# Two layers of graph attention with norms: bank copies, norms and statistics in another order in the first steps and in the tail

## The chip, the cores and the metric

The kernel runs on one core of a Trainium2 chip. The metric is the device time in microseconds (us) of that core, as a median of several runs. TensorE (PE in the profile) multiplies matrices, VectorE (DVE), ScalarE (ACT) and GpSimd (POOL) compute elementwise, and SyncE (SP) issues nearly all transfers (DMAs) between SBUF and DRAM. PE writes its products to banks of a memory called PSUM; the other engines read them from there.

## The reference

The input x has 128 batch elements of 128 rows and 512 columns, in fp32. Cut to what matters, with adj used as both weights of layer 0:

```python
A = einsum('od,bdn->bon', adj, x); C = A + b
x = layernorm(x + max(relu(A[:, :, None, :] + (C - A)[:, :, :, None]), axis=-1))
q, k, v = split_heads(x @ w_qkv)            # 8 heads of 64
attn = softmax(where(adj == 0, -inf, q @ k.T / 8))
o = (attn @ v) @ w_proj + b_proj
ln = layernorm(o) * gamma + beta
out = layernorm(x + o + ln)
```

In layer 0, C - A is the bias alone, so the kernel needs only the row maximum of adj @ x, plus bias, with relu, added to x.

## The kernel before, in words

Two batch elements make a pair and a step; four make a group (G = 4, 32 groups of 512 rows). All arithmetic is in fp32. The three large products (q and k, v, the projection) are made by a scheme of seven block products in place of eight for a pair of 2 by 2 blocks. `Unit` (L153) holds one such product: `product(i)` issues the 8 matmul instructions in the profile of product i into one of four PSUM banks b1 to b4. Products 1, 6 and 7 accumulate in b1; `snap(k)` (L171) copies b1 to SBUF on ACT after each of them, and the next product into b1 waits for that copy. `result(half, col)` (L176) adds a snap and a bank on DVE: (0, 0) takes b2 and snap 1, (0, 1) b3 and snap 2, (1, 1) b3 and snap 3, (1, 0) b4 and snap 3. Product 5 opens b3 and product 3 adds to it, so product 3 waits until result (1, 1) has read b3, and the next unit's product 5 waits until result (0, 1) has read it.

Every instruction is issued in the order in which the code is written (`tc.keep_in_program_order`, L71): each engine has one queue in that order, and an instruction waits at its head until all that it needs is done. There is no scheduler; the order is written out by hand. The helpers `pe` (L73) and `tt` (L76) record all matmuls under L74 and all elementwise two-operand operations under L77.

Layer 0 for element f: `l0_mm` (adjacency matmul into a whole bank), `l0_max` (DVE maximum and r), `l0_add` (ACT), statistics, `l0_norm` (ACT). `bn` (L233) makes two DVE instructions per element, L235 and L236. `finish_stats` (L238) makes one DVE instruction (sh, L244) and three on POOL: variance plus epsilon (L246), a power of -0.5 which gives rs, and the product of sh and rs. `normalize` (L252) is one ACT instruction, L254, that needs both. `stats` (L603) does bn for each item and one finish for all. The normed x is transposed in 32 by 32 blocks on DVE (`l0_transpose`), written to DRAM and read back in another order (`l0_write`, `l0_read`: four SP transfers each; `xhop`, `x1T`), gets beta added on POOL (`l0_beta`) and is spilled to DRAM for the end.

Attention for element b: `scores` (PE), `softmax_max` (DVE), `softmax_exp` (ACT, one head at a time), `softmax_div` and `prob_transpose` (DVE, tiles s and pu), `prob_write` and `prob_read` (SP: one write to `hop`, four reads into pT), `attend` (PE, into banks po and pa), `attend_copy` (ACT, to oT).

The first steps, L612 to L697, are written out: the units qk(0, 0), called `before` from L656 on, and qk(0, 1), called `cur` from L659, with the layer 0 work of elements 4 to 9. The loop at L706 takes p from 0 to 60. Step p makes a unit `first` and a unit `second`, layer 0 for later pairs, attention for pair p, and the tail of earlier pairs; p = 0 has branches of its own, where `first` is the v unit of group 0.

After the loop (L860 on) the rest is written out, with L = 127 the last element. Its last lines, L934 to L1030, are the tail of the last elements. The tail for element t on the usual way: `tail_inner_one` (L580, ACT norm of o), `tail_residual_one` (L584, three POOL operations: times gamma, plus o, plus the spilled x), statistics of z, and `tail_outer_one` (L598, ACT norm and the store). `tail_fused` (L589) replaces inner norm and residual by three DVE instructions, L594, L595 and L77, of which the second needs rs. For L - 3 to L, o is left in PSUM by `last_project` (L499); o of the others lies in SBUF. Before, L - 3 to L take the fused way and L - 11 to L - 4 the usual one.

Of the kernel before, what the change touches and what calls it, by code (L numbers as in the profile page):

```python
# [16 lines left out]
def kernel(  # L17
# [35 lines left out]
    G = 4  # L53
    GT = G * P
    HT = GT // 2
    HE = D // 2
# [28 lines left out]
    def broadcast(queue, name, src):  # L85
        t = const.tile([P, D], F32, name=name)
        pin(queue.dma_start(out=t, in_=src.partition_broadcast(P)))
        return t
# [26 lines left out]
    def weight_sums(w, cols, width):  # L115
        t = w[:, :, :, ds(cols, width)]
        b11, b21, b22, b12 = (t[:, i] for i in range(4))
        tt(nc.gpsimd, t[:, 4], b12, b11, ALU.subtract)
        tt(nc.gpsimd, t[:, 6], b22, b12, ALU.subtract)
        tt(nc.gpsimd, t[:, 5], b22, t[:, 4], ALU.subtract)  # L120
        tt(nc.gpsimd, t[:, 3], b21, t[:, 5], ALU.subtract)
# [111 lines left out]
    def bn(src, mv, k):  # L233
        st = small.tile([P, 6], F32, tag="st", name=f"st_{k}_{mv.name}")
        pin(nc.vector.bn_stats(st, src))  # L235
        pin(nc.vector.bn_aggr(mv[:, k], st))  # L236
# [37 lines left out]
    def l0_norm(f):  # L274
        normalize(xs[f], xs[f], ("y", f))
# [133 lines left out]
    def softmax_div(b):  # L409
        rec = small.tile([P, H], F32, tag="rec", name=f"rec_{b}")  # L410
        pin(nc.vector.reciprocal(rec, psums.pop(b)))  # L411
        p = prob[b]
        tt(nc.vector, p, p, rec.unsqueeze(2).to_broadcast([P, H, P]), ALU.mult)
# [52 lines left out]
    def attend_copy(b):  # L466
        g, h, jj = place(b)
        if jj == 0:
            tag = "x" if (g, h) == (NG - 2, 0) else "oT"
            oT[g, h] = sb.tile([P, KC, HT], F32, tag=tag, name=f"oT_{g}_{h}", bufs=2)  # L470
        pin(nc.scalar.copy(oT[g, h][:, :, ts(jj, P)], pos.pop(b)))
# [45 lines left out]
    def o_of(b):  # L517
        g, h, jj = place(b)
        return os_[b] if b in os_ else os_[g, h][:, jj]
# [60 lines left out]
    def tail_inner_one(b):  # L580
        z_tile(b)
        normalize(zs[b], o_of(b), ("o", b))
# [20 lines left out]
    def stats(name, *items):  # L603

        mv = small.tile([P, NC, 2], F32, tag="mv", name=f"mv_{name}")
        for k, (kind, b) in enumerate(items):
            bn({"o": o_of, "z": zs.get, "y": xs.get}[kind](b), mv, k)
        finish_stats(mv, items)
        return mv
# [51 lines left out]
    weight_load(wp, w_proj, 0, HE, 0, HE)  # L661
    ga_bc = broadcast(nc.sync, "ga_bc", ln_gamma)
    bp_bc = broadcast(nc.sync, "bp_bc", b_proj)
    before.snap(3)
    before.result(1, 1)
    before.result(1, 0)
    stats("second", *(("y", f) for f in range(G, 2 * G)))
    weight_sums(wv, 0, HE)
    for f in range(G, G + 2):
        l0_norm(f)  # L670
    cur.product(2)
    cur.product(1)
    cur.snap(1)
    cur.result(0, 0)
    before.product(3)
    before.result(0, 1)
    for f in range(G + 2, 2 * G):
        l0_norm(f)
    cur.product(6)
    cur.snap(2)  # L680
    cur.product(5)
# [24 lines left out]
    for p in range(LAST + 1):  # L706
# [7 lines left out]
        keys = []  # L714
# [79 lines left out]
            l0_read(n)  # L794
        if p > 0:
            first.snap(3)
        softmax_div(b)
        prob_transpose(b)
        prob_write(b)
        prob_read(a)  # L800
        prob_read(b)
        first.result(1, 1)
        first.result(1, 0)
        if ph == 1 and tb is not None:
            one("z", zs, tb)
        if ph == 0 and ta is not None:
# [53 lines left out]
    L = B - 1  # L860
# [101 lines left out]
    o_u.result(0, 0)  # L962
    v_u.product(3)
    v_u.result(0, 1)
    for t in range(L - 11, L - 7):
        tail_residual_one(t)
    o_u.product(6)
    softmax_exp(L, range(4))
# [14 lines left out]
    tail_outer(B // 2 - 7)  # L983
    tail_store(B // 2 - 7)
    mv = small.tile([P, NC, 2], F32, tag="mv", name="mv_last_2")
    keys = [("z", L - 11), ("z", L - 10), ("o", L - 5), ("o", L - 4), ("o", L - 7), ("o", L - 6)]
    bn(zs[L - 11], mv, 0)
    bn(zs[L - 10], mv, 1)
    o_u.result(1, 1)
    o_u.result(1, 0)  # L990
    bn(o_of(L - 5), mv, 2)
    bn(o_of(L - 4), mv, 3)
    o_u.product(3)
    o_u.result(0, 1)
    last_project(L - 3, wlast, "b2")
    last_project(L - 2, wlast, "pss0")
    attend(L - 1)
    attend_copy(L - 1)
    attend(L, "pa")
    attend_copy(L)  # L1000
    last_project(L - 1, wlast, "pss1")
    last_project(L, wlast, "b1")
    bn(o_of(L - 7), mv, 4)
    bn(o_of(L - 6), mv, 5)
    finish_stats(mv, keys)
    for t in (L - 5, L - 4, L - 7, L - 6):
        tail_inner_one(t)
    for t in (L - 11, L - 10):
        tail_outer_one(t)
    tail_residual_one(L - 5)  # L1010
    mv = stats("last_3", ("o", L - 3), ("o", L - 2), ("z", L - 9), ("z", L - 8))
    tail_residual_one(L - 4)
    for t in (L - 9, L - 8):
        tail_outer_one(t)
    tail_fused(L - 3, mv[:, 0, 0:1])
    tail_fused(L - 2, mv[:, 1, 0:1])
    mv = stats("last_4", ("o", L - 1), ("z", L - 3), ("z", L - 2))
    tail_residual_one(L - 7)
    tail_fused(L - 1, mv[:, 0, 0:1])
    for t in (L - 3, L - 2):  # L1020
        tail_outer_one(t)
    mv = stats("last_5", ("o", L), ("z", L - 5), ("z", L - 4))
    tail_residual_one(L - 6)
    tail_fused(L, mv[:, 0, 0:1])
    for t in (L - 5, L - 4):
        tail_outer_one(t)
    stats("last_6", ("z", L - 1), ("z", L - 7))
    stats("last_7", ("z", L), ("z", L - 6))
    for t in (L - 1, L - 7, L, L - 6):
        tail_outer_one(t)  # L1030


# [39 lines left out]
```

## Time and profile before

| what | value |
|---|---|
| median of 3 runs | 1987.33 us (1987.06 to 1987.37) |
| profiled execution, its own time | 1988.53 us |
| span of that execution | 1986.7 us |
| PE busy | 1946.4 us (98%) |
| DVE busy | 1565.2 us (79%) |
| POOL busy | 1293.7 us (65%) |
| ACT busy | 1055.1 us (53%) |
| PE in the chain that ended last | 95% |

Times in the trace count from the start of the span. A timeline row gives start, length, engine, line, operation, output and inputs, count, and in brackets how long the engine was idle before it and which instruction released it. Rows of several instructions are merged, so a length can hold small gaps. `SPq` is SP's own queue: the length is that of issuing, not of the transfer. The span is a little shorter than the execution's own time, which also holds what lies around the span.

### The profile page before, as it was taken

What the parts mean: (1) busy time and instruction counts of PE and PEld (TensorE: products, weight loads), DVE (VectorE), ACT (ScalarE), POOL (GpSimd) and SP (SyncE); (2) the same over time, 40 slices, a digit from 0 to 9 for tenths busy, and PEclk for the clock granted to TensorE, in tenths of its full rate; (3) what the DMA queues carried; (4) which work ended last, traced back from release to release, by engine and by line L of the source; (5) the groups of instructions that cost most, each with busy time, mean ns of one, the idle gap of its engine ahead of it and who ended that gap; (6) DMA issues with size and microseconds to landing.
All of it is one profiled execution on the core that took longest, in us unless ns stands there. A gap on an engine that the chain in (4) does not pass through costs nothing.

```text
span 1986.7 us, 33036 instructions
## 1 busy us (share of the span) xinstructions
PE 1946.4 (98%) x11545; PEld 1644.8 (83%) x11545; DVE 1565.2 (79%) x2518; ACT 1055.1 (53%) x3066; POOL 1293.7 (65%) x808
## 2 busy tenths in 40 slices
PE   7999999999999999999999999999999999999994
PEld 5888888888888888888888888888888888888872
DVE  5668788788788788787787787787787787787685
ACT  3435546546556556555555555555455455455453
POOL 5246667677667677667676667676667676676646
PEclk8999999999999999999999999999999999999997
DMA  5665576675675675765766765765766766765553
GB/s 191 145 170 139 159 195 155 181 195 153 183 187 158 186 187 157 187 170 169 192 168 169 194 165 164 202 165 164 202 159 168 198 164 165 198 162 158 159 177 121
DMA packets 445655, 341.76 MB, mean 172 GB/s; under 512 B 276912, under 2 KB 378416, under 8 KB 445488
## 3 DMA queue, kind: packets, MB, share of 16 engines
q1 hardware_dynamic: 445056, 338.85, 64.1%
q8 instruction: 92, 1.51, 0.3%
q10 hardware_dynamic: 432, 0.79, 0.1%
q14 instruction: 75, 0.61, 0.1%
HBM read 172.82 MB, written 166.72 MB: 171 GB/s over the span
## 4 chain that ended last, share of the span: by engine, by line
PE 95%; DVE 2%; DMA 1%; POOL 1%; ACT 0%; issue 0%; SPq 0%; ACTq 0%; POOLq 0%; DVEq 0%
PE b_qk L74 39%; PE b_v L74 19%; PE b_o L74 19%; PE pss L74 6%; PE po L74 6%; PE pa L74 5%; PE pp L74 0%; POOL zl L77 0%; DMA x<-in_x_dram 0%; DMA wqk<-in_L_gnn_w_qkv_dram 0%; DVE s_x L77 0%; DMA hop<-pu 0%; DVE st_mv_last L235 0%; DVE z L77 0%; POOL rs_mv_last L77 0%
## 5 line engine op out<-in xcount | busy, mean ns | idle before, releaser
L74 PE MATMUL b_qk<-s_x,wqk 128*128 128x256 f32 x2048 | 476.3, 381 | 4.0 <-ACT u_qk L173 3.9
L74 PEld LDWEIGHTS b_qk<-s_x,wqk 128*128 128x128 f32 x2048 | 391.8, 191 | 58.1 <-POOL wv L77 4.3
L400 ACT ACTIVATE s<-s,nmax 128x128 f32<-128x128 f32 x1024 | 396.2, 391 | 6.7 <-DVE nmax L393 6.7
L74 PE MATMUL b_qk<-x1T,wqk 128*128 128x256 f32 x1536 | 360.7, 385 | 0.8 <-DVE x1T L299 0.8
L74 PEld LDWEIGHTS b_qk<-x1T,wqk 128*128 128x128 f32 x1536 | 288.7, 191 | 45.5 <-DVE x1T L299 1.2
L77 POOL TENSOR_TENSOR z<-z,ga_bc 128x1024 f32<-128x1024 f32 x58 | 164.6, 2838 | 168.4 <-ACT z L254 168.4
L246 POOL TENSOR_SCALAR rs_mv<-mv 128x6 f32<-128x6 f32 (+2 forms) x61 | 14.6, 240 | 380.2 <-DVE mv L236 380.2
L77 DVE TENSOR_TENSOR s<-s,rec 128x1024 f32<-128x1024 f32 x128 | 252.3, 1971 | 4.4
L173 ACT COPY u_qk<-b_qk 128x512 f32<-128x512 f32 x192 | 112.3, 585 | 248.2 <-PE b_qk L74 247.2
L74 PE MATMUL b_v<-wv,s_x 128*128 128x256 f32 x1024 | 237.2, 380 | 2.0 <-DVE v L179 2.0
L74 PE MATMUL b_o<-wp,s_o 128*128 128x256 f32 x992 | 230.2, 380 | 0.5 <-DVE v L179 0.5
L74 PEld LDWEIGHTS b_v<-wv,s_x 128*128 128x128 f32 x1024 | 194.8, 190 | 28.7 <-DVE v L179 2.4
L179 DVE TENSOR_TENSOR qk<-b_qk,u_qk 128x512 f32<-128x512 f32 x256 | 168.1, 675 | 62.2 <-PE b_qk L74 44.6
L381 DVE SCALAR_TENSOR_TENSOR s<-pss,mask 128x512 f32<-128x512 f32 x256 | 164.3, 684 | 59.5 <-PE pss L74 59.1
L74 PEld LDWEIGHTS b_o<-wp,s_o 128*128 128x128 f32 x992 | 188.5, 190 | 26.7 <-DVE v L179 0.9
L77 POOL TENSOR_TENSOR x<-x,be_bc 128x1024 f32<-128x1024 f32 x64 | 182.1, 2847 | 34.0 <-DVE rec L411 27.6
L400 ACT ACTIVATION_READ_ACCUMULATOR s<-s,nmax 128x1 f32 x1024 | 194.2, 190 | 0.0
L179 DVE TENSOR_TENSOR v<-b_v,u_v 128x512 f32<-128x512 f32 x128 | 87.0, 681 | 133.6 <-PE po L74 128.8
L173 ACT COPY u_o<-b_o 128x512 f32<-128x512 f32 x93 | 54.4, 585 | 247.3 <-PE b_o L74 247.3
L173 ACT COPY u_v<-b_v 128x512 f32<-128x512 f32 x96 | 56.2, 585 | 238.5 <-PE b_v L74 238.5
L74 PE MATMUL b_v<-wv,x1T 128*128 128x256 f32 x768 | 176.3, 379 | 0.0
L74 PEld LDWEIGHTS b_v<-wv,x1T 128*128 128x128 f32 x768 | 146.3, 190 | 31.9 <-issue 13.8
(107 smaller groups left out, 3395.5 us busy)
## 6 DMA issues: line engine op xcount, KB each, us to landing
hop<-pu SPq DMA_DIRECT2D x128, 512.0 KB, 3.5
pT<-hop SPq DMA_DIRECT2D x512, 128.0 KB, 3.7
spill<-x SPq DMA_DIRECT2D x64, 512.0 KB, 4.8
x<-in_x_dram SPq DMA_DIRECT2D x62, 512.0 KB, 4.4
xhop<-xt SPq DMA_DIRECT2D x248, 128.0 KB, 2.3
x1T<-xhop SPq DMA_DIRECT2D x248, 128.0 KB, 3.9
xr<-spill SPq DMA_DIRECT2D x59, 512.0 KB, 3.6
out_dram<-xr SPq DMA_DIRECT2D x58, 512.0 KB, 4.1
```

Of the source, the lines that this page charges most:

```text
L74: pin(nc.tensor.matmul(*args, **kwargs))
L77: pin(eng.tensor_tensor(dst, a, b, op))
L173: pin(nc.scalar.copy(t, self.banks[1]))
L179: nc.vector.tensor_tensor(self.out[half, col], self.banks[bank], self.snaps[k], ALU.add)
L246: pin(nc.gpsimd.tensor_scalar(rs[:, :n], mv[:, :n, 1], EPS, None, ALU.add))
L381: nc.vector.scalar_tensor_tensor(s[:, par], pss[b][par], SCALE, mask.unsqueeze(1).to_broadcast([P, NP, P]), ALU.mult, ALU.add,)
L400: nc.scalar.activation(prob[b][:, i], prob[b][:, i], AF.Exp, bias=nmax[b][:, i : i + 1], accum_out=psums[b][:, i : i + 1],)
```

## The change

In the first steps, the statistics of elements 4 to 7 and the sums of the v weights move ahead of the old unit's last copy and two results; the four norms of these elements, which stood two by two ahead of the copies `cur.snap(1)` and `cur.snap(2)`, now stand together between these copies. At p = 0, results (1, 1) and (1, 0) of the v unit move ahead of the softmax divisions, behind which they stood.

In the tail, elements L - 4 and L - 6 go from the usual way to the fused one, so that six elements take it in place of four. Residual L - 8 moves behind the first finish. The statistics are finished in seven portions of 4, 3, 3, 3, 4, 1 and 2 columns in place of six of 6, 4, 3, 3, 2 and 2. The inner norms of L - 5 and L - 7 and the outer ones of L - 11, L - 10 and L - 9 stand ahead of the attention copies of L - 1 and L on ACT; all of these stood behind the copies before. The order on PE is the same in both kernels; that on SP differs only in the order and tiles of the last stores.

```diff
--- before.py
+++ after.py
@@ -661,21 +661,19 @@
     weight_load(wp, w_proj, 0, HE, 0, HE)
     ga_bc = broadcast(nc.sync, "ga_bc", ln_gamma)
     bp_bc = broadcast(nc.sync, "bp_bc", b_proj)
+    stats("second", *(("y", f) for f in range(G, 2 * G)))
+    weight_sums(wv, 0, HE)
     before.snap(3)
     before.result(1, 1)
     before.result(1, 0)
-    stats("second", *(("y", f) for f in range(G, 2 * G)))
-    weight_sums(wv, 0, HE)
-    for f in range(G, G + 2):
-        l0_norm(f)
     cur.product(2)
     cur.product(1)
     cur.snap(1)
     cur.result(0, 0)
     before.product(3)
+    for f in range(G, 2 * G):
+        l0_norm(f)
     before.result(0, 1)
-    for f in range(G + 2, 2 * G):
-        l0_norm(f)
     cur.product(6)
     cur.snap(2)
     cur.product(5)
@@ -794,13 +792,17 @@
             l0_read(n)
         if p > 0:
             first.snap(3)
+        else:
+            first.result(1, 1)
+            first.result(1, 0)
         softmax_div(b)
         prob_transpose(b)
         prob_write(b)
         prob_read(a)
         prob_read(b)
-        first.result(1, 1)
-        first.result(1, 0)
+        if p > 0:
+            first.result(1, 1)
+            first.result(1, 0)
         if ph == 1 and tb is not None:
             one("z", zs, tb)
         if ph == 0 and ta is not None:
@@ -962,7 +964,7 @@
     o_u.result(0, 0)
     v_u.product(3)
     v_u.result(0, 1)
-    for t in range(L - 11, L - 7):
+    for t in range(L - 11, L - 8):
         tail_residual_one(t)
     o_u.product(6)
     softmax_exp(L, range(4))
@@ -983,50 +985,51 @@
     tail_outer(B // 2 - 7)
     tail_store(B // 2 - 7)
     mv = small.tile([P, NC, 2], F32, tag="mv", name="mv_last_2")
-    keys = [("z", L - 11), ("z", L - 10), ("o", L - 5), ("o", L - 4), ("o", L - 7), ("o", L - 6)]
+    keys = [("z", L - 11), ("z", L - 10), ("o", L - 5), ("o", L - 4)]
     bn(zs[L - 11], mv, 0)
     bn(zs[L - 10], mv, 1)
     o_u.result(1, 1)
     o_u.result(1, 0)
     bn(o_of(L - 5), mv, 2)
     bn(o_of(L - 4), mv, 3)
+    finish_stats(mv, keys)
+    tail_inner_one(L - 5)
+    for t in (L - 11, L - 10):
+        tail_outer_one(t)
+    tail_residual_one(L - 8)
     o_u.product(3)
     o_u.result(0, 1)
     last_project(L - 3, wlast, "b2")
     last_project(L - 2, wlast, "pss0")
     attend(L - 1)
+    attend(L, "pa")
+    mv2 = stats("last_3", ("o", L - 7), ("o", L - 6), ("z", L - 9))
+    tail_inner_one(L - 7)
+    tail_outer_one(L - 9)
+    tail_residual_one(L - 5)
+    tail_fused(L - 4, mv[:, 3, 0:1])
     attend_copy(L - 1)
-    attend(L, "pa")
     attend_copy(L)
     last_project(L - 1, wlast, "pss1")
     last_project(L, wlast, "b1")
-    bn(o_of(L - 7), mv, 4)
-    bn(o_of(L - 6), mv, 5)
-    finish_stats(mv, keys)
-    for t in (L - 5, L - 4, L - 7, L - 6):
-        tail_inner_one(t)
-    for t in (L - 11, L - 10):
+    mv = stats("last_4", ("o", L - 3), ("z", L - 8), ("z", L - 4))
+    tail_residual_one(L - 7)
+    for t in (L - 8, L - 4):
         tail_outer_one(t)
-    tail_residual_one(L - 5)
-    mv = stats("last_3", ("o", L - 3), ("o", L - 2), ("z", L - 9), ("z", L - 8))
-    tail_residual_one(L - 4)
-    for t in (L - 9, L - 8):
+    tail_fused(L - 6, mv2[:, 1, 0:1])
+    mv2 = stats("last_5", ("o", L - 2), ("z", L - 6), ("z", L - 5))
+    tail_fused(L - 3, mv[:, 0, 0:1])
+    for t in (L - 6, L - 5):
         tail_outer_one(t)
-    tail_fused(L - 3, mv[:, 0, 0:1])
-    tail_fused(L - 2, mv[:, 1, 0:1])
-    mv = stats("last_4", ("o", L - 1), ("z", L - 3), ("z", L - 2))
-    tail_residual_one(L - 7)
+    tail_fused(L - 2, mv2[:, 0, 0:1])
+    mv = stats("last_6", ("o", L - 1), ("z", L - 3), ("z", L - 2), ("z", L - 7))
+    for t in (L - 3, L - 2, L - 7):
+        tail_outer_one(t)
+    mv2 = stats("last_7", ("o", L))
     tail_fused(L - 1, mv[:, 0, 0:1])
-    for t in (L - 3, L - 2):
-        tail_outer_one(t)
-    mv = stats("last_5", ("o", L), ("z", L - 5), ("z", L - 4))
-    tail_residual_one(L - 6)
-    tail_fused(L, mv[:, 0, 0:1])
-    for t in (L - 5, L - 4):
-        tail_outer_one(t)
-    stats("last_6", ("z", L - 1), ("z", L - 7))
-    stats("last_7", ("z", L), ("z", L - 6))
-    for t in (L - 1, L - 7, L, L - 6):
+    tail_fused(L, mv2[:, 0, 0:1])
+    stats("last_8", ("z", L - 1), ("z", L))
+    for t in (L - 1, L):
         tail_outer_one(t)
 
 
```

## Prediction

> **What bounds the kernel now.** First I read the span and busy table: TensorE (PE) is busy 98% of 1986.7 us, so a change off its queue can only pay where PE waits, or after its last matmul. The waits of PE list every such place:
>
> ```profile
> PE b_qk L74 <- ACT u_qk L173: 3.9, 1, 3.9
> ...
> PE b_v L74 <- DVE v L179: 2.0, 1, 2.0
> ...
> PE po L74 <- DMA pT<-hop: 1.0, 1, 1.0
> ```
>
> The columns are total, number and longest wait in us. The other entries lie before 19 us, but for one of 0.5. So from 80 us to 1928 us PE never waits: what is won before stays won. The 3.9 us wait and what follows, in a table by stretch (busy time of PE, PE weight load, DVE, ACT, POOL, then granted clock, DMA share, GB/s):
>
> ```profile
> 40.00:44.00 4.00, 1.34 (x7) 0.84 (x5) 1.50 (x5) 0.85 (x2) 2.35 (x4) 1.00 0.68 248
> 44.00:48.00 4.00, 2.72 (x7) 2.22 (x8) 2.83 (x5) 2.56 (x4) 3.92 (x4) 0.53 0.02 4
> 48.00:52.00 4.00, 4.00 (x12) 3.14 (x11) 0.85 (x2) 0.58 (x1) 4.00 (x3) 0.62 0.82 202
> ```
>
> After the wait the clock is 0.53, then 0.62. The ACT timeline shows why PE waits (start, length, idle before in brackets):
>
> ```profile
> 43.15 1.52 ACT L254 ACTIVATE x<-x,sh_mv_second,rs_mv_second 128x512 f32<-128x512 f32 x2 [6.27 <-POOL sh_mv_second L77]
> 44.57 0.56 ACT L173 COPY u_qk<-b_qk 128x512 f32<-128x512 f32 x1
> ```
>
> The bank copy PE needs stands behind two norms, which waited 6.27 us for statistics. PE's timeline and SP's around the 2.0 us wait:
>
> ```profile
> 78.41 2.00 PE L74 MATMUL b_v<-wv,s_x 128*128 128x256 f32 x8 [1.99 <-DVE v L179]
> ```
>
> ```profile
> 73.58 0.34 SPq L430 DMA_DIRECT2D hop<-pu  x1
> 74.03 3.43 SPq L318 DMA_DIRECT2D x1T<-xhop  x4
> 77.81 0.38 SPq L430 DMA_DIRECT2D hop<-pu  x1
> 78.23 4.91 SPq L441 DMA_DIRECT2D pT<-hop  x8
> ```
>
> Last the tail. PE's last matmul ends at 1962.6, 24 us before the end. VectorE (DVE) and GpSimd (POOL) there:
>
> ```profile
> 1959.99 0.75 DVE L595 SCALAR_TENSOR_TENSOR z<-z,rs_mv_last,pp 128x512 f32<-128x512 f32 x1 [5.21 <-POOL rs_mv_last L77]
> 1960.77 1.24 DVE L77 TENSOR_TENSOR z<-z,wlast 128x512 f32<-128x512 f32 x1
> ```
>
> ```profile
> 1954.69 1.27 POOL L77 TENSOR_TENSOR zl<-zl,ga_bc 128x512 f32<-128x512 f32 x1 [7.97 <-ACT zl L254]
> ```
>
> Both idle before the tail's heavy part: POOL 7.97 us, because the inner norms stand on ACT behind the attention copies, DVE 1.85, 3.77 and 5.21 us, the last because rs stands on POOL behind three residual operations. Then DVE runs 21 us almost without a gap to 1980.9.
>
> **What the Trainium skill says.** "TensorE: Matmul & The Clock Gate", "What's actually happening": an idle window of about 3.4 us halves the PE clock, and about as much busy time restores it. The trace agrees: 16 matmuls after the 3.93 us wait took 6.54 us, where 16 take 3.45 (at 53.53); after 1.99 us the clock stayed 1.00. "SBUF — State Buffer", "Who interferes with whom": a DVE instruction with two SBUF inputs and a GpSimd one reading SBUF exclude each other for a whole instruction. The trace agrees: DVE's 1.24 us add at 1960.77 began under a POOL operation that ended at 1961.47 and ended 0.54 after it. "DMA: Bandwidth & Descriptors", "Two DMAs through the same engine are not ordered": a DMA that reads what another wrote has to wait for its completion. Here SP waits up to 1.1 us for hop writes.
>
> **First step (L664 to L681): bank copies ahead of norms.** Four statistics (0.80 us each) now run on DVE from 35.62, when the last r ends, to 38.82; they need ACT's additions, done by 36.2. The two result additions follow: the one that product 3 of the old unit waits for ends near 39.6, where PE could start at 39.45: 0.2 us lost. Product 3 (8 matmuls, 1.73) ends at 41.4. The copy of bank 1 needs product 1, ended 39.6, and no longer waits for norms: 40.25. Product 6 runs at once to 43.1. The old unit's last result follows product 3, 42.2, so product 5 runs to 44.85 and the two adjacency matmuls start there instead of at 51.65: **6.8 us** = 3.9 wait + 3.1 slow clock - 0.2. The moved norms: POOL gives sh at 40.5 (1.63 after the statistics), four norms take 3.0 to 43.55, and the copy after product 6 follows at 44.1, product 7 needing it only at 48.3. Transposes and their 16 DMAs on SP come 4 us earlier. POOL's weight sums (5.07) and two beta additions (4.65) end at 50.2, 0.45 late for the third statistics; that norm has 0.4 us to spare before the next copy, so nothing is paid.
>
> **Step p = 0 (L787 to L803): two results ahead of softmax division.** All times 6.8 earlier. Copy 3 ends at 65.1; the results end at 65.75 and 66.4. PE reaches product 3 at 69.6 and does not wait: 2.0 us more. But division and transposition of a now end at 69.1 (66.8 without the move), exp b ends at 68.2, and b's transposition ends at 71.85. After it come the maxima, and then the result that product 5 of the next unit waits for: 74.15 against PE's 73.1, a new wait of 1.1. On SP the hop of a is issued at 69.1 and the four x1T reads hold the queue 3.9 us, so b's hop goes out at 73.0, 4.8 earlier than before. Before, the last pT read was issued 4.9 after that hop and landed some 3.8 later, at 86.5, where PE wanted it at 88.2. Now it lands near 81.7; PE arrives at 80.25 and waits 1.4. Gain left: 88.2 - 81.7 = **6.5 us**. This DMA decides here; the 1.1 us wait lies inside it. Bounds: 3.5 (a later landing and part of the slow clock) to 8.9 (6.8 + 2.0, no wait).
>
> **Tail, on the clock of before.** PE's order is the same: o of L-3, L-2, L-1, L are complete at 1946.65, 1951.35, 1957.95, 1962.65. The first statistics shrink from six to four and do not wait for L-7 and L-6: DVE has them at 1940.9, POOL finishes (four columns, 1.63) at 1942.55, then residual L-8 (3.97) to 1946.5, then the next finish (three columns, 1.48) to 1948.0. ACT does inner L-5 and outer L-11, L-10 by 1944.85, inner L-7 and outer L-9 by 1949.5; attention copy L-1 cannot start before 1952.5, so the norms ahead of it cost nothing (2.8 us spare). SP's added early stores are behind the last pT reads.
>
> DVE now runs from 1942.25 nearly without idle: 16 statistics at 0.80 = 12.8, six fused tails (two more: L-4 and L-6) of 0.77 + 0.77 + 0.65 = 13.1, six sh of 0.1. That alone ends at 1969.4. A fused tail whose o is in SBUF is not in the trace of before: its first two operations may take 0.75 each as with PSUM, or up to 1.27 more each if POOL is reading. I placed POOL's residuals L-5 (1948.3 to 1952.4) and L-7 (1954.5 to 1958.6) beside fused L-4 and L-6 and charge 0.9 + 2.4 us of lock waits. In steps: fused L-4 ends 1948.5, statistics 1951.0, fused L-6 1956.0, statistics 1958.5, fused L-3 and L-2 1962.7 (their rs are ready at 1953 to 1960), five statistics 1966.9, fused L-1 and L 1971.2, two statistics 1972.8. Then POOL's finish for two columns 1.28, two ACT norms 1.6, and as before 3.07 from the last norm to the end of the span: 1978.75. Gain 1986.7 - 1978.75 = **7.9 us**. Bounds: 11.3 without lock waits, 3.6 if each of the six two-SBUF operations waits a whole POOL operation (7.6 us in place of 3.3). PE or attend needs no cover there.
>
> **Sum.** 6.5 + 7.9 = 14.4: span 1972.3, with the 1.83 us around the span (1988.53 - 1986.7) 1974.1 for a profiled execution. That one stood 1.2 above the median of the runs, 1987.33, which becomes **1972.9**.
>
> **Rivals.** (1) DVE and POOL block each other in the tail: for it, DVE is then the bound and s<-s,rec took 2.12 us beside POOL at 1929.27 (1.23 at 1922.78); against it, POOL's residuals fall from eight to six. Tail 3.6, total 10.1: 1977.2. (2) The pT transfer takes the place of the removed waits: for it, SP is held by x1T reads ahead of b's hop; if it lands 2 us later still, PE idles over 3.4 us and pays the 3.1 us of slow clock again. Early gain 6.5 - 2.0 - 3.1 = 1.4, total 9.3: 1978.0. (3) Slower: attention copies L-1 and L stand behind inner L-7 and outer L-9 on ACT, and those behind POOL's residual L-8. If POOL finishes the statistics after 1950.8, PE's last two projections slip; o of L has a further 3.3 us before DVE wants it (1966.0 against 1962.65). It decides from 6.1 us of lateness and makes the kernel slower only from 6.1 + 14.4 = 20.5; at 25 us late: 1991.8. Against it: POOL had waits to spare. (4) The order has no effect because other waits stand in the same places: 1987.
>
> **Chances.** Forecast 0.73, alone within 1969.5 to 1976.5; (1) 0.12; (2) 0.08; (3) 0.04; (4) 0.03. The range runs from 1968.5 (a gain near the upper bounds in both halves) to 1978.0 (rival 2). 0.2% is 4 us, about what a measurement here tells from no change: the forecast, (1) and (2) are beyond it: faster 0.93, same 0.03, slower 0.04.
>
> **What would show it.** PE's 3.9 us wait gone and the clock 1.00 from 40 to 52 us; the adjacency matmuls at 44.9. The 2.0 us wait for v gone, new waits near 73 us (about 1) and for pT near 80 us (about 1.4). DVE nearly without idle from 1936 (1942.3 less 6.5), 16 us between PE's last matmul and the end in place of 24. Wrong if PE waits longer than 3.4 us anywhere, if PE waits for oT copies in the tail, or if DVE idles there for rs.

## The result and the profile after

| | before | after |
|---|---|---|
| median | 1987.35 us (1987.06 to 1988.32, 4 runs) | 1973.76 us (1972.93 to 1975.04, 4 runs) |
| profiled execution, own time | 1988.53 us | 1973.78 us |
| span of it | 1986.7 us | 1972.0 us |

The ratio is 0.9931, with a 95% interval of 0.9914 to 0.9949: 13.6 us faster, where 1972.9 had been forecast. The sum was nearly right, its three stretches were not. The spans, cut at two marks that both traces have (step 1's `scores`, and `attend` of L), give:

| stretch | before | after | gain | forecast |
|---|---|---|---|---|
| start to step 1's scores | 89.14 | 81.33 | 7.81 | 6.5 |
| from there to attend of L | 1862.17 | 1860.92 | 1.25 | 0 |
| attend of L to the end | 35.39 | 29.75 | 5.64 | 7.9 |

PE's waits (total, number, longest) in the changed kernel. Of the three that the prediction showed none is left; the last line is what stands in place of the 2.0 us wait for v:

```profile
PE b_qk L74 <- DVE x1T L299: 0.8, 1, 0.8
...
PE b_o L74 <- DVE v L179: 0.5, 1, 0.5
...
PE b_qk L74 <- DVE v L179: 0.2, 1, 0.2
```

The table by stretch, for the same 12 us as before (PE, weight load, DVE, ACT, POOL, then the granted clock): PE is full and the clock stays 1.00, where it had been 0.53 and 0.62.

```profile
40.00:44.00 4.00, 3.96 (x19) 3.49 (x19) 3.20 (x7) 3.60 (x6) 3.92 (x5) 1.00 0.81 280
44.00:48.00 4.00, 4.00 (x17) 2.76 (x16) 2.71 (x7) 0.98 (x2) 3.92 (x3) 1.00 0.74 187
48.00:52.00 4.00, 4.00 (x20) 3.54 (x19) 3.15 (x7) 1.54 (x4) 3.73 (x5) 1.00 0.96 183
```

ACT's timeline shows how: the bank copy that began at 44.57 behind two norms now stands at 40.12, and the four norms run behind it while PE has work.

```profile
40.12 0.59 ACT L173 COPY u_qk<-b_qk 128x512 f32<-128x512 f32 x1 [2.83 <-PE b_qk L74]
40.99 2.93 ACT L254 ACTIVATE x<-x,sh_mv_second,rs_mv_second 128x512 f32<-128x512 f32 x4 [0.28 <-POOL sh_mv_second L77]
43.83 0.59 ACT L173 COPY u_qk<-b_qk 128x512 f32<-128x512 f32 x1
```

At p = 0, PE's timeline and then SP's. The wait for v is 0.24; on SP a's hop goes out at 67.28 and b's at 71.52:

```profile
73.82 1.99 PE L74 MATMUL b_qk<-s_x,wqk 128*128 128x256 f32 x8 [0.24 <-DVE v L179]
```

```profile
67.28 0.34 SPq L430 DMA_DIRECT2D hop<-pu  x1
67.73 3.42 SPq L318 DMA_DIRECT2D x1T<-xhop  x4
71.52 0.34 SPq L430 DMA_DIRECT2D hop<-pu  x1
71.91 5.06 SPq L441 DMA_DIRECT2D pT<-hop  x8
```

The tail, first DVE and then POOL, at the first of the two new fused tails. DVE has no idle time from 1931 to 1966, and POOL none from 1933.2 to 1953.9:

```profile
1936.45 0.94 DVE L244 TENSOR_SCALAR sh_mv_last<-mv_last 128x3 f32<-128x3 f32 x1
1937.30 0.74 DVE L594 SCALAR_TENSOR_TENSOR zl<-o,mv_last,ga_bc 128x512 f32<-128x512 f32 x1
1938.16 1.56 DVE L595 SCALAR_TENSOR_TENSOR zl<-zl,rs_mv_last,o 128x512 f32<-128x512 f32 x1
1939.75 0.69 DVE L77 TENSOR_TENSOR zl<-zl,wlast 128x512 f32<-128x512 f32 x1
```

```profile
1936.10 1.26 POOL L77 TENSOR_TENSOR zl<-zl,o 128x512 f32<-128x512 f32 x1
1937.44 1.73 POOL L77 TENSOR_TENSOR zl<-zl,wlast 128x512 f32<-128x512 f32 x1
1939.14 0.68 POOL L246 TENSOR_SCALAR rs_mv_last<-mv_last 128x3 f32<-128x3 f32 x1
1939.90 1.27 POOL L77 TENSOR_TENSOR rs_mv_last<-rs_mv_last,mhalf 128x3 f32<-128x3 f32 x1
```

The two lists read as one. DVE's sh of three columns ends at 1937.39, when POOL's addition (1936.10 + 1.26) ends at 1937.36. POOL's next addition begins while DVE's L594 runs and takes 1.73 where 1.27 is usual. DVE's L595 meets that one: 1.56 where 0.75 is usual. POOL's addition of epsilon meets L595: 0.68 where 0.23 is usual. They take turns.

### The profile page after: what moved, and what is told of

Same layout as the page of the kernel before. It is cut to its first block, busy times and chain, and to the rows that moved or that the text cites. A ratio compares the mean times of both kernels' runs of the same rounds, so it can differ in the third digit from the quotient of the medians.

```text
span 1972.0 us, 33041 instructions
## 1 busy us (share of the span) xinstructions
PE 1942.3 (98%) x11545; PEld 1639.0 (83%) x11545; DVE 1571.9 (80%) x2525; ACT 1054.0 (53%) x3064; POOL 1289.7 (65%) x805
## 4 chain that ended last, share of the span: by engine, by line
PE 96%; DVE 2%; POOL 1%; DMA 1%; ACT 0%; issue 0%; ACTq 0%; POOLq 0%; SPq 0%; DVEq 0%
PE b_qk L74 40%; PE b_v L74 19%; PE b_o L74 19%; PE pss L74 6%; PE po L74 6%; PE pa L74 5%; POOL zl L77 1%; DMA be_bc<-in_L_gnn_ln_beta_dram 0%; POOL rs_mv_last L77 0%; DVE st_mv_last L235 0%; DMA wqk<-in_L_gnn_w_qkv_dram 0%; DVE s_x L77 0%; ACT s L400 0%; DVE s L381 0%; DVE pu L421 0%
## 5 line engine op out<-in xcount | busy, mean ns | idle before, releaser
L77 POOL TENSOR_TENSOR z<-z,ga_bc 128x1024 f32<-128x1024 f32 x58 | 164.7, 2839 | 168.3 <-ACT z L254 168.3
L246 POOL TENSOR_SCALAR rs_mv<-mv 128x6 f32<-128x6 f32 (+2 forms) x61 | 14.7, 241 | 380.9 <-DVE mv L236 380.9
L77 DVE TENSOR_TENSOR s<-s,rec 128x1024 f32<-128x1024 f32 x128 | 252.8, 1975 | 4.4
L179 DVE TENSOR_TENSOR qk<-b_qk,u_qk 128x512 f32<-128x512 f32 x256 | 168.1, 675 | 56.9 <-PE b_qk L74 44.8
L77 POOL TENSOR_TENSOR x<-x,be_bc 128x1024 f32<-128x1024 f32 x64 | 182.3, 2850 | 33.4 <-DVE rec L411 27.3
L179 DVE TENSOR_TENSOR v<-b_v,u_v 128x512 f32<-128x512 f32 x128 | 87.0, 680 | 133.7 <-PE po L74 128.9
L74 PEld LDWEIGHTS b_v<-wv,x1T 128*128 128x128 f32 x768 | 145.9, 190 | 32.2 <-issue 13.6
```

Of the source, the lines that this page charges most:

```text
L74: pin(nc.tensor.matmul(*args, **kwargs))
L77: pin(eng.tensor_tensor(dst, a, b, op))
L179: nc.vector.tensor_tensor(self.out[half, col], self.banks[bank], self.snaps[k], ALU.add)
L246: pin(nc.gpsimd.tensor_scalar(rs[:, :n], mv[:, :n, 1], EPS, None, ALU.add))
```

## The experiments

The medians of the kernel before, run beside them, were 1987.06 us (the first four kernels of the table), 1987.17 (the next four) and 1986.85 (the last four). Diffs are against the changed kernel unless another is named. Single profiles with the same first steps differ by up to 3.2 us in the first 48 us alone: after the start PE's clock is at half for 6.83 us in nine of the fourteen profiles and for 10.24 us in five (e2_steps, e5_stats, e10_shact, e12_four, e13_ballast). So stretches that begin later are compared.

| kernel | median us (range, runs) | ratio to before, 95% interval |
|---|---|---|
| e1_first: first step alone | 1981.92 (1979.99 to 1983.05, 11) | 0.9973, 0.9964 to 0.9982 |
| e2_steps: first step and p = 0 | 1978.78 (1978.70 to 1981.49, 5) | 0.9965, 0.9953 to 0.9978 |
| e3_tail: tail alone | 1981.17 (1980.35 to 1982.54, 7) | 0.9970, 0.9959 to 0.9981 |
| e4_copies | 1982.48 (1981.13 to 1985.75, 13) | 0.9978, 0.9970 to 0.9986 |
| e5_stats | 1983.52 (1981.55 to 1986.22, 14) | 0.9981, 0.9973 to 0.9989 |
| e6_div | 1976.14 (1975.27 to 1976.17, 5) | 0.9942, 0.9930 to 0.9955 |
| e8_l4pool | 1975.91 (1975.30 to 1978.21, 5) | 0.9944, 0.9931 to 0.9956 |
| e9_peadd | 1970.47 (1969.72 to 1972.68, 4) | 0.9917, 0.9903 to 0.9930 |
| e10_shact | 1974.17 (1973.27 to 1976.61, 5) | 0.9935, 0.9922 to 0.9947 |
| e11_both | 1971.41 (1970.95 to 1972.35, 4) | 0.9920, 0.9907 to 0.9934 |
| e12_four | 1977.03 (1976.19 to 1979.15, 5) | 0.9950, 0.9936 to 0.9963 |
| e13_ballast | 1982.20 (1981.44 to 1984.51, 10) | 0.9977, 0.9968 to 0.9986 |

### The three parts by themselves

**e1_first** is the first hunk alone: the branches at p = 0 and the whole tail are those of before. Its diff against before:

```diff
+    stats("second", *(("y", f) for f in range(G, 2 * G)))
+    weight_sums(wv, 0, HE)
     before.snap(3)
     before.result(1, 1)
     before.result(1, 0)
-    stats("second", *(("y", f) for f in range(G, 2 * G)))
-    weight_sums(wv, 0, HE)
-    for f in range(G, G + 2):
-        l0_norm(f)
...
     before.product(3)
+    for f in range(G, 2 * G):
+        l0_norm(f)
     before.result(0, 1)
-    for f in range(G + 2, 2 * G):
-        l0_norm(f)
```

> The first-step part alone, on the kernel before. Theory (the parts act in their own places and add up): PE's 3.9 us wait and the slow clock go, the adjacency matmuls start 6.7 us earlier for the same start of the kernel, the 2.0 us wait for v at p = 0 stays, the tail stays 24 us long: 1987.3 - 6.7 = 1980.6. Rival (the gain is given back later, at the transfers of p = 0 or in the loop): the matmuls start as early, but step 1's scores gain under 5 us and the kernel stands at 1982.5 or above.

Measured 1981.92, between the two. From product 3 of the old unit to the adjacency matmuls it takes 5.28 us, as in the changed kernel (5.28), against 12.20 before: 6.9 us, as forecast. But from the second adjacency matmuls to the first attention product it takes 17.85, against 16.16 before. The wait for v is the same 2.00; the clock behind it is not. The table by stretch of this kernel (columns as above):

```profile
72.00:74.00 2.00, 2.00 (x8) 1.59 (x7) 1.55 (x4) 1.07 (x2) 0.00 (x0) 0.61 1.12 353
74.00:76.00 2.00, 2.00 (x7) 1.61 (x6) 1.80 (x3) 0.38 (x1) 1.27 (x1) 0.53 1.03 219
```

So the 2 us wait, which cost no clock before, here costs 1.7 us of it as well.

**e2_steps** adds the second hunk; only the tail is that of before. Its diff against e1_first:

```diff
         if p > 0:
             first.snap(3)
+        else:
+            first.result(1, 1)
+            first.result(1, 0)
         softmax_div(b)
...
-        first.result(1, 1)
-        first.result(1, 0)
+        if p > 0:
+            first.result(1, 1)
+            first.result(1, 0)
```

> The first-step part and the p = 0 part, without the tail part. Theory: as with the whole change up to the loop, so the 2.0 us wait for v is replaced by one of 0.2 us; step 1's scores come 8.2 us earlier for the same start of the kernel, and the end too: 1987.3 - 8.2 = 1979.1. If the pT wait of 1.0 us in the last part also goes, 1978.1; that would show that it hangs on when PE gets there and not on the tail part. Rival: nothing over the first-step part alone, 1980.6, because b's probabilities then land late.

Measured 1978.78, as the theory had it, but by another sum: from the second adjacency matmuls to attention takes 14.40, which is 3.45 less than in e1_first, not the 1.75 that the same step gains against before. The executions fall into two groups, 1978.7 and 1981.4; the profiled one is of the second, with its adjacency matmuls at 47.3 where the changed kernel has them at 45.35, so the difference lies in the start. The edits don't touch its half-speed time, but they make it dearer: at 37.31 this execution is 0.90 us behind the changed kernel's (36.41), and at product 3 (42.03 against 40.07) 1.96. Product 3 waits 0.73 us there for result (1, 1), which now stands on DVE behind the four statistics; in the changed kernel's own profile it waits 0.2.

**e3_tail** is the tail hunks alone (the first two undone as in e1_first and e2_steps, read backwards).

> The tail part alone. Theory: from the end of PE's last matmul to the end of the span 18.4 us in place of 24.1, nothing else moves: 1987.3 - 5.7 = 1981.6; with the pT wait of 1.0 us gone, 1980.6. Rival (the prediction's own sum for the tail): 16.1 us from the last matmul, 1979.4.

Measured 1981.17, with the theory. PE's last matmul ends 18.44 us before the end of the span (18.42 in the changed kernel, 24.06 before). From step 1's scores to attend of L this kernel takes 1861.2, e1_first and e2_steps 1860.9, before 1862.2: the wait of 1.0 us for pT at 1938 us, which the prediction shows among PE's waits, is in the profile of before alone and in none of the thirteen others, neither in those with the old first step nor in those with the old tail. So it is put down to that one execution, which stood 1.2 us above the median of its runs; the kernel before was profiled only once. The parts add up: -8.3 (e2_steps) and -5.9 (e3_tail) make -14.2, against -13.6 for the whole.

### What in the first step pays

**e4_copies** leaves the statistics where before had them, behind the two results; the norms go behind the copy as in the change. It has the p = 0 and the tail of before, as has e5_stats.

```diff
-    stats("second", *(("y", f) for f in range(G, 2 * G)))
-    weight_sums(wv, 0, HE)
     before.snap(3)
     before.result(1, 1)
     before.result(1, 0)
+    stats("second", *(("y", f) for f in range(G, 2 * G)))
+    weight_sums(wv, 0, HE)
```

> Of the first-step part only the order on ACT (all four norms behind the bank copy and behind product 3), with the statistics left behind the two results as before. Theory: the copy ahead of the norms is all that counts; the norms start at 43.2 and end at 46.1, the copy after product 6 follows by 46.7, and product 7 wants it only at 48.3, so the time equals that of the whole first-step part, 1980.6, to within 0.5. Rival: the later norms delay the transposes, the third statistics or POOL, and PE waits 1 us or more again: 1981.6 or above.

Measured 1982.48: neither value exactly, nearer the rival. Product 3 to the adjacency matmuls takes 5.22, so the copies do the whole of it. But the later statistics aren't free: the norms end later, and so do POOL's beta additions; the sh of the third statistics meets one and takes 2.29 us on DVE, and PE then waits 0.8 us for a v copy. From the first adjacency matmuls to the scores it takes 13.43, against 12.17 in e1_first: 1.26.

**e5_stats** does the reverse: statistics early, norms still two by two ahead of the copies.

```diff
+    for f in range(G, G + 2):
+        l0_norm(f)
     cur.product(2)
     cur.product(1)
     cur.snap(1)
     cur.result(0, 0)
     before.product(3)
-    for f in range(G, 2 * G):
-        l0_norm(f)
     before.result(0, 1)
+    for f in range(G + 2, 2 * G):
+        l0_norm(f)
```

> Of the first-step part only the statistics ahead of the two results, the norms left ahead of the bank copies. The copy then waits for two norms that start at about 40.5, so PE still waits, but some 1.3 us in place of 3.9. Theory (the slow clock depends on how a wait falls against a free-running window, so a short wait mostly goes free): 6.6 us from the start of product 3 to the adjacency matmuls, against 12.2 before and 5.3 with the whole change, clock 1.00 there; in all 1982.5. Rival (any wait there costs a full window at half speed): 8.3 us between these points.

Measured 1983.52 and 6.56 us from product 3 to the adjacency matmuls, the theory's 6.6. PE still waits 1.0 us for the bank copy behind the norms, but the clock stays 1.00. Early statistics alone thus remove most of the 6.9 us (5.6): the wait shrinks from 3.9 to 1.0, and no clock is lost behind it. The order of copies and norms adds 1.3. It, too, pays the clock behind the 2.00 us wait (17.84 to attention), hence a time 1 us over the theory's 1982.5.

### The 2 us wait and the clock

**e13_ballast** is e1_first with PE kept busy ahead of product 3 of p = 0. The eight added matmuls make a product that nobody uses.

```diff
+        if p == 0:
+            junk = psum.tile([P, D], F32, tag="po", name="junk")
+            for _ in range(8):
+                pe(junk[:, :HE], lhsT=ident, rhs=ga_bc[:, :HE], start=True, stop=True)
         first.product(3)
```

> The first step of the change alone (1981.92), with eight matmuls more whose product nobody uses (identity by gamma, into the bank po), put on PE ahead of product 3 of p = 0, where PE waits 2.00 us for v. Theory (the 2.0 us of idleness make the clock fall there): the wait falls to 0.2 to 0.3, the clock stays 1.00 from 68 to 78 us, and from the second adjacency matmuls to attend takes 16.2 in place of 17.85: 1980.2. Rival (the clock falls there for another reason, such as how long PE had run): 17.8 and 1981.9.

The eight matmuls took 3.45 us (16 records), twice what I had reckoned, so the time, 1982.20, can't speak: they cover the wait and run 1.3 us beyond it. The same two stretches in the trace of this kernel:

```profile
72.00:74.00 2.00, 2.00 (x11) 1.75 (x11) 2.00 (x3) 0.00 (x0) 0.00 (x0) 1.00 1.23 151
74.00:76.00 2.00, 2.00 (x11) 1.77 (x10) 1.71 (x5) 0.91 (x2) 0.00 (x0) 1.00 1.17 331
```

The clock stays 1.00 from 64 to 80 us, and the stretch to attention takes 17.34, although product 3 begins 1.3 us later in it than after e1_first's wait (17.85). That fits idleness as the cause, but by itself it shows little, for in before and in e3_tail the clock stayed 1.00 behind the same 2.00 us wait.

What decides can be read from the times at which the clock changes. In each of the fourteen traces, up to 100 us, all changes of the granted clock lie a whole number of 3.413 us apart: in before at 16.91, 23.73, 44.21 and 51.04 (2, 6 and 2 times 3.413), in e1_first at 14.42, 21.25, 72.45 and 75.86 (2, 15 and 1 times). "TensorE: Matmul & The Clock Gate", "What's actually happening", of the Trainium skill says that the windows of some 3.4 us are free-running and aren't reset when a kernel starts, and the traces agree. On this grid, the window that holds the wait:

| profile | window | PE busy in it | clock in the next |
|---|---|---|---|
| before | 74.93 to 78.35 | 1.49 of 3.41 us | 1.00 |
| e3_tail | 72.74 to 76.15 | 2.05 | 1.00 |
| e1_first | 69.04 to 72.45 | 1.41 | 0.50 |
| e4_copies | 70.26 to 73.67 | 1.42 | 0.50 |
| e5_stats | 72.45 to 75.86 | 1.42 | 0.50 |
| e13_ballast | 68.78 to 72.19 | 3.41 | 1.00 |

Where the whole wait lay in one window, the next one ran at half speed, which cost the 1.7 us (half of 3.41); where a boundary cut the wait, nothing was lost. In before it was a near thing: the boundary cut off 0.07 us. The limit, here between 1.42 and 1.49 us of work, holds for this place alone (behind PE's last matmuls in e6_div the clock fell after a window with PE busy for 2.20 us), and no run moved the wait within the window on purpose. A short wait doesn't mostly go free, as e5_stats's theory had it: its 1.0 us wait did (PE busy 1.99 in that window), its 2.0 us wait not.

The long wait of the first step shows the same. In before the clock was at half for two windows behind it (44.21 to 51.04), in e3_tail, where the wait is as long (3.94), for one (45.43 to 48.85). Product 3 to the adjacency matmuls takes 11.05 us in e3_tail, so against that execution the first hunk gains 5.8 us and not 6.9.

### The step at p = 0

**e6_div** is the changed kernel with the two results of p = 0 ahead of a's softmax division as well as b's.

```diff
             first.snap(3)
             softmax_exp(b)
+            first.result(1, 1)
+            first.result(1, 0)
         softmax_div(a)
...
         if p > 0:
             first.snap(3)
-        else:
-            first.result(1, 1)
-            first.result(1, 0)
```

> The changed kernel, but with the two results of p = 0 ahead of the softmax division of a, as the prediction took the change to be, and not between the divisions of a and b, where it has them. Theory (the prediction's step was right for that order): b's hop is issued 1.5 to 2 us later than in the changed kernel, PE waits about 1.1 us before product 5 and about 1.4 us for pT, and from the first adjacency matmuls to step 1's scores it takes 37.6 us in place of 36.0: 1973.8 + 1.6 = 1975.4. Rival (the order of these few instructions does not matter, the transfers have time to spare): within 0.3 of the changed kernel, 1973.8.

The prediction reckoned with this order; the change has the results between a's division and b's (see below). Measured 1976.14, somewhat over the theory's 1975.4 and clear of the rival. Its PE waits are the ones that the prediction had listed for the change, about 1.1 and 1.4:

```profile
PE po L74 <- DMA pT<-hop: 1.6, 2, 1.3
PE b_qk L74 <- DVE v L179: 1.0, 1, 1.0
```

From the first adjacency matmuls to step 1's scores it takes 38.39, against 35.98 in the changed kernel: 2.4 us.

### What bounds the tail

**e8_l4pool** puts one element, L - 4, back on the usual way (ACT norm, three POOL operations), with five fused.

```diff
     tail_inner_one(L - 5)
+    tail_inner_one(L - 4)
...
-    tail_fused(L - 4, mv[:, 3, 0:1])
+    tail_residual_one(L - 4)
...
-    mv = stats("last_4", ("o", L - 3), ("z", L - 8), ("z", L - 4))
+    mv = stats("last_4", ("o", L - 3), ("z", L - 8))
...
-    mv2 = stats("last_5", ("o", L - 2), ("z", L - 6), ("z", L - 5))
+    mv2 = stats("last_5", ("o", L - 2), ("z", L - 6), ("z", L - 5), ("z", L - 4))
```

> The changed kernel with L - 4 on the usual way again (five fused tails, seven residuals), its statistics one portion later. It moves 4 us of work from DVE, some 3 us there, to POOL. Theory (in the tail POOL ends last until the fifth portion's rs at 1953.7, and DVE waits for it): the tail from PE's last matmul to the end grows from 18.4 to about 21.5, 1976.9 in all. Rival (the prediction's view, DVE is the bound throughout): it shrinks to about 15.5, 1970.9.

Slower, as the theory had it, by less than it said: PE's last matmul ends 20.58 us before the end, 2.16 more than in the changed kernel (3.1 expected). DVE has three operations less and stands idle for POOL, 2.65 us for a residual and 1.80 for rs. So the tail is not DVE's sum alone.

**e12_four** puts L - 6 back as well: the order and portions of the change with the four fused tails of before.

```diff
+    tail_inner_one(L - 4)
+    tail_inner_one(L - 6)
...
-    tail_fused(L - 4, mv[:, 3, 0:1])
+    tail_residual_one(L - 4)
...
-    tail_fused(L - 6, mv2[:, 1, 0:1])
...
+    tail_residual_one(L - 6)
...
-    stats("last_8", ("z", L - 1), ("z", L))
+    stats("last_8", ("z", L - 6), ("z", L - 1), ("z", L))
```

> The changed kernel in its order and portions, but with only four fused tails, L-3 to L, as in the kernel before: L-4 and L-6 go the usual way again (ACT norm, three POOL operations), residual L-6 last on POOL. Theory: the tail's gain of 5.6 us is the fusing, since POOL is full to 1954 us, and one element put back took 2.2 of it: two take 4.0 to 4.8, time 1977.8 to 1978.6. Rival (the order and the portions bring it; DVE, which is relieved of 3.05 us for each element put back, ends earlier): 1974 to 1976.

1977.03 lies between the two. From attend of L to the end it takes 32.95 us, against 35.39 before, 31.91 in e8_l4pool and 29.75 in the changed kernel. Both of my readings were too simple: of the 5.6 us, order and portions bring 2.4, the first fused element (L - 6) 1.0 and the second (L - 4) 2.2. DVE's longest waits for POOL in this kernel:

```profile
1949.64 0.69 DVE L235 BATCH_NORM_STATS2 st_mv_last<-zl 128x6 f32<-128x512 f32 x1 [3.00 <-POOL zl L77]
...
1956.32 0.75 DVE L595 SCALAR_TENSOR_TENSOR z<-z,rs_mv_last,pp 128x512 f32<-128x512 f32 x1 [1.66 <-POOL rs_mv_last L77]
```

**e10_shact** asks whether the three long sh of DVE (0.94, 1.17 and 1.09) are a cost of their own. ACT, which has time, makes them.

```diff
+        if "last" in mv.name:
+            pin(nc.scalar.activation(sh[:, :n], mv[:, :n, 0], AF.Identity, scale=-1.0))
+        else:
+            pin(nc.vector.tensor_scalar(sh[:, :n], mv[:, :n, 0], -1.0, None, ALU.mult))
-        pin(nc.vector.tensor_scalar(sh[:, :n], mv[:, :n, 0], -1.0, None, ALU.mult))
```

> The changed kernel with the tail's sh (mean times -1, L244) made on ACT in place of DVE. Three of these took 0.94, 1.17 and 1.09 us on DVE in the changed kernel, beside POOL operations, against some 0.17. Theory: between 1933 and 1954 us DVE and POOL are both without idle time and hold each other, so that taking the sh away only moves the wait: the next DVE operation (L594 or L595) meets the same POOL operation, or waits for POOL's rs. Gain at most 0.6 us: 1973.2 or more. Rival (the tail is DVE's sum alone, and the six sh are the term that was mis-sized): the three sh give back what they took over 0.1, and 0.1 each for all: gain 2.9 to 3.5, 1970.3 to 1970.9.

1974.17, no gain over 1973.76. DVE's timeline of this kernel shows where the time went (L597 and L598 are the changed kernel's L594 and L595):

```profile
1939.78 1.57 DVE L597 SCALAR_TENSOR_TENSOR zl<-o,mv_last,ga_bc 128x512 f32<-128x512 f32 x1
...
1946.09 1.80 DVE L597 SCALAR_TENSOR_TENSOR zl<-o,mv_last,ga_bc 128x512 f32<-128x512 f32 x1
...
1956.84 0.75 DVE L598 SCALAR_TENSOR_TENSOR z<-z,rs_mv_last,pp 128x512 f32<-128x512 f32 x1 [0.41 <-POOL rs_mv_last L77]
```

The operation behind the missing sh, 0.74 us in the changed kernel, meets the same POOL addition and takes 1.57 and 1.80. Where the third sh is gone, the addition L77 behind it takes 1.54 in place of 0.69, and DVE waits for rs. DVE's run from the statistics of L - 7 to the last ones takes 31.2 us against 31.9: 0.7 us won, a little over the theory's 0.6, and far from the rival's 2.9 to 3.5, which falls.

The medians don't show the 0.7 us, because the edit also costs time ahead of the tail. Its test of the name moves the sh of the first of the last portions as well (six columns), and there it puts this sh, which waits for statistics, ahead of a bank copy on ACT. The copy in the changed kernel, 0.16 us after attention begins on PE (1908.59), and then here, 2.06 us after (1910.81):

```profile
1908.75 0.59 ACT L173 COPY u_v<-b_v 128x512 f32<-128x512 f32 x1 [3.11 <-PE b_v L74]
```

```profile
1912.75 0.21 ACT L245 ACTIVATE sh_mv_last<-mv_last 128x6 f32<-128x6 f32 x1 [4.88 <-DVE mv_last L236]
1912.87 0.57 ACT L173 COPY u_v<-b_v 128x512 f32<-128x512 f32 x1
```

From step 1's scores to attend of L it takes 1862.15 us in place of 1860.92. It is the order that the first step of the change had cured.

### A faster version

**e9_peadd** takes the third DVE operation (plus x) of L - 3 to L away: PE adds x to o in PSUM by a matmul with the identity, and the first fused operation, which must come before it, follows the statistics at once.

```diff
+    def fused_first(b, mean):
+        z_tile(b)
+        pin(nc.vector.scalar_tensor_tensor(zs[b], o_of(b), mean, ga_bc, ALU.subtract, ALU.mult))
+        pe(o_of(b), lhsT=ident, rhs=rs_.pop(b), start=False, stop=True, skip_group_check=True)
+
+    def fused_second(b):
+        z, rs = zs[b], stat_of.pop(("o", b))[0]
+        pin(nc.vector.scalar_tensor_tensor(z, z, rs, o_of(b), ALU.mult, ALU.add))
...
-    tail_fused(L - 1, mv[:, 0, 0:1])
-    tail_fused(L, mv2[:, 0, 0:1])
+    fused_first(L, mv2[:, 0, 0:1])
+    fused_second(L - 1)
+    fused_second(L)
```

> The changed kernel with the spilled x of L - 3 to L added to o in PSUM by TensorE, by a matmul with the identity, after the statistics and the first fused instruction have read o; the third fused instruction of these four is gone, and the first one stands right behind the statistics. PE gets four matmuls more while it is idle or nearly so. Theory (after 1953.7 the tail is a chain of DVE instructions, and before that DVE has some 1.4 us of waits): three or four adds of 0.65 go from the chain and two first instructions move into the wait, so the end comes 3.5 us earlier, 1970.3. Rival (POOL's rs of the fifth portion sets the pace, and PE's adds delay o of L): 1 us earlier at most, 1972.8.

1970.47, the theory's value: faster than both kernels. Attend of L to the end takes 26.4 us, 3.36 less. PE has the time for it: nothing waits for three of the four additions, and for that of L DVE waits 0.64 us. PE's timeline of this kernel has one of them at

```profile
1950.34 1.12 PE L74 MATMUL pp<-wlast,ident 128*128 128x512 f32 x2 [1.13 <-DVE z L600]
```

**e11_both** is e9_peadd with sh on ACT as in e10_shact.

> The earlier experiment in which PE adds x of L-3 to L in PSUM (1970.47), and sh on ACT as well. Its sh on DVE took 0.93, 1.17, 0.36 and 0.19 in the tail. Theory: only the second, ahead of an operation that reads PSUM, is won, and part of it goes into the next wait: 0.2 to 1.0 gained, 1969.5 to 1970.3. Rival (DVE's sum alone): 2.2 gained, 1968.3.

1971.41, so nothing is gained (0.9920 against 0.9917). In the trace attend of L to the end falls by 0.6 us, to 25.8, within the theory's 0.2 to 1.0, but the sh ahead of the tail costs here what it costs in e10_shact (1862.15 us from step 1's scores to attend of L). With sh on ACT in the tail alone the kernel may be faster; no run shows it. e9_peadd stays the fastest.

## Why the prediction was right, and where it was not

**Bank copies ahead of norms: right.** Forecast were 6.8 us at the adjacency matmuls. Measured are 6.9 from product 3 on, less 0.2 by which product 3 waits for result (1, 1) behind the statistics, as forecast: 6.7. Product 3 began 0.62 later than in before; the other 0.4 is the start of that execution (36.41 for 36.00 one product earlier). In the sum 3.9 + 3.1 - 0.2 the slow clock is a little too large: the 16 matmuls took 6.37 us from start to start, where 16 take 3.45, which makes 2.9 (the 6.54 of the prediction holds the end of the last one too). e5_stats shows both parts: with the wait shortened to 1.0 the slow clock goes as well. Each half of the edit would have done most of it alone (5.6 by the statistics, 7.0 by the copies), which the prediction didn't say. The 0.45 us by which POOL would be late for the third statistics cost nothing, as said; e4_copies, where it is later, pays 1.26. Some 1.15 us of the 6.9 hang on how the wait fell on the clock's windows in this one profile of before (see e3_tail's 11.05 above).

**Results at p = 0: misread.** "Two results ahead of softmax division" holds for b's division only. In the code the branch stands behind `softmax_div(a)`, `prob_transpose(a)` and `prob_write(a)`; the section on the change, too, says "divisions" where it should say the second one. From the wrong place followed a's division at the wrong time, and from that every later number: a's hop at 69.1 (measured 67.28), b's at 73.0 (71.52), a wait of 1.1 for v (0.24), one of 1.4 for pT (about 0.2). The working itself was sound, as e6_div shows: the order assumed gives waits of 1.0 and 1.6. From the adjacency matmuls to step 1's scores the forecast had a loss of 0.3 us (6.8 to 6.5), and a gain of 1.5 was measured (6.3 to 7.81), 1.8 us more than forecast; the two orders differ by 2.4 us in the runs. (The upper bound of this part, 6.8 + 2.0, is 8.8 and not 8.9.)

**What the 2.0 us wait costs: undersized.** It was put at 2.0 of idleness without a loss of clock, on the one profile of before. That it cost no clock there was luck, by 0.07 us of the window. In the three profiles with a changed first step and the old p = 0 the clock falls (e1_first, e4_copies, e5_stats), so that behind the changed first step the second hunk takes away 3.45 us (17.85 to 14.40; 3.1 in the medians), though against before it shows as 1.75.

**The tail: oversized by 2.3 us.** Attend of L is 9.06 earlier than before (1942.25 for 1951.31). Shifted by that, the forecast has the end at 1969.7; it was 1972.0. DVE's run, term by term (a lock wait is the time by which an operation is longer beside one of the other engine):

| term | forecast | measured | late |
|---|---|---|---|
| DVE's run begins | 1933.19 | 1933.92 | 0.73 |
| 16 statistics | 12.8 | 13.36 | 0.56 |
| five sh with the gap ahead of each | 0.5 | 3.52 | 3.02 |
| six fused tails, lock waits in them | 13.1 + 3.3 | 15.05 | -1.35 |
| other waits | 0.85 | 0 | -0.85 |
| from the last statistics to the end | 5.95 | 6.14 | 0.19 |

The first row and the fifth nearly cancel. At 1933.19 DVE begins a result addition, L179 (0.69), and only behind it the statistics; and the terms that the prediction names end at 1968.75, where it writes 1969.4. The 0.65 us over, counted here among the other waits, may be that addition.

The step that failed is "six sh of 0.1", and more widely that lock waits were charged to DVE's six two-SBUF operations only. "SBUF — State Buffer", "Who interferes with whom", of the Trainium skill counts tensor_scalar, with its one SBUF input, among the operations that exclude GpSimd when they run in a two-port mode. L244 behaves so here: three columns took 0.94, 1.17 and 1.09 beside a POOL operation and ended within 0.03 us of its end each time; four columns took 0.17 with no such operation beside them. Whether DVE ran in such a mode the traces don't say. And POOL's own operations wait for DVE's: 0.46 in each of the two additions that meet L594, 0.45 in each addition of epsilon that meets L595, and a power of three columns takes 1.27 to 1.35 where 0.87 was seen. e10_shact then says how to read such rows: of the 3 us only 0.7 came back without sh. While both engines are full and exclude each other, whichever operation comes next pays. Rival (1), the two engines blocking each other, was thus a part of the truth; its size, 4.3 us off the tail's gain, was 1.9 times too large.

**No cover needed for the attention copies: right.** The norms moved ahead of them end at 1943.0, and the first copy begins at 1943.44 right behind its product. ACT had 0.45 us to spare, not 2.8.

**The wait for pT at 1938 us: overlooked as chance.** Left in the sum at nothing, it went by itself: the 1.25 us of the middle stretch come, as far as the other profiles show, from the execution of before that was profiled, not from the change. In the medians it can't be seen, and they show 13.6 where the spans show 14.7.

So the span's gain came out at 14.7 for 14.4 because +1.8 (p = 0), -0.5 (0.4 the later start of that execution, 0.1 the copies), +1.25 (that wait) and -2.3 (tail) nearly cancel. The first step was understood; that the sum came so near was luck.

## What to carry to other kernels

Look for engine queues in which a short copy that TensorE waits for stands behind work that waits for something else: putting it first won 6.9 us against one profile here and 5.8 against another, of which 2.9 and 1.8 were slow clock; and when e10_shact brought such an order back elsewhere, it lost 1.2. Count a TensorE wait of even 2 us as possibly costing clock, since five profiles with the same wait show both, by how it fell on the 3.41 us windows. Where VectorE and GpSimd are both full, moving one small operation off an engine hands most of its wait to the next (3.2 us of sh taken away, 0.7 won); what pays is to take whole operations to an engine with time to spare, as the addition of x on TensorE did (3.3 us).

## What was not expected of the hardware

- The changes of TensorE's granted clock lay on a grid of 3.413 us in every trace, placed differently in each. The same 2.00 us of idleness left the clock at 1.00 in the two profiles in which a grid line cut it, and brought it to 0.50 for one window in the three in which none did, for 1.7 us.
- A VectorE operation on 128x3 elements took 0.94 to 1.17 us beside GpSimd, and one on 128x2 took 2.29 in e4_copies, where it began under a GpSimd addition of 128x1024 and ended 0.02 us after it. On four columns, with no long GpSimd operation beside it, it took 0.17.
- A matmul of 128x128 by 128x256 from SBUF with the identity appears as two records; eight took 3.45 us (e13_ballast). One of 128x512 took 1.12 (e9_peadd).
- GpSimd's power takes 0.57 us for one column, 0.72 for two, 0.87 for three (in e10_shact; the others in the changed kernel) and 1.04 for four.
